# Gate and up projections of twelve feed-forward units in pairs: seven outer products over both token shares, each an inner set of seven on quarters

## The chip, the core and the metric

One core of a Trainium2 chip runs the whole decoder layer in one launch. The metric is the device time of that launch in microseconds (us), the median of several runs. TensorE (PE in the profile) multiplies matrices, VectorE (DVE) and ScalarE (ACT) work on what it leaves in PSUM, and SyncE (SP) issues nearly all DMAs from one queue in order.

## The reference

The input `x` has 2 sequences of 512 tokens of width 1024, all float32. With `ln` for a layer norm, the layer computes

```
x = ln(x + attention(x))      # 32 query heads, 8 key/value heads of 128, sliding window of 128
x = ln(x + fake_quant(x) @ fake_quant(ctx))        # "cross": ctx is 1024 x 1024 for each sequence
gate, up = (x/128) @ w_gate.T, (x/128) @ w_up.T    # 2752 hidden rows
inter = trunc(clip(silu(gate) * up * 128, -128, 127))
out = ln(x + trunc(clip((inter @ w_down.T) * 128, -128, 127)))
```

## The kernel before

**Stages.** The profile shows three. From 0 to about 790 us are the q, k and v projections and attention, for one key/value head group `g` after another (8 groups, some 98 us each). From 790 to 1170 us is the output projection (`project_out`), with the cross stage behind it. From 1170 us to the end is `feed_forward`.

**Strassen sets.** Each large projection is done by `strassen`: a 2x2 block product in seven products instead of eight. `left` holds seven weight factors (blocks and sums of blocks), `right` seven activation factors. A `product` is a chain of four matmuls (`KH` = 4 chunks of 128 of the inner dimension, 256 columns each) into one PSUM bank. The seven are made in the order 1, 5, 6, 2, 7, 4, 3 in four banks, `one` to `four`, and combined by four ACT copies and three DVE adds, of which the last, of `c12`, frees the bank `three` that the second product of the next set writes.

**Feed-forward units.** The hidden rows are cut into 21 units `m` of 128 and a rest of 64. The 1024 tokens are cut into two shares of 512 (`SHARES`: first the later tokens of both sequences, then the earlier ones). The loop takes the 22 units on share 0, then the 22 on share 1. For a unit on a share one Strassen set gives gate and up (the two block rows are the gate rows and the up rows of the unit, the two block columns are halves of the share); `activate` makes the whole-numbered activations on ACT and DVE; `split` (ACT) and `rest_of_split` (DVE) cut the down weights into two parts `hi` and `lo`, so that `down` can run in the one-pass format fp32r; and `down` adds two units (share 0) or four (share 1) to `acc` by matmuls of 512 columns and one DVE add per token tile and half. The last eight units are held and projected at the end.

**Background work in attention.** The weight factors that are sums do not depend on the tokens. A generator (`ahead`) makes them during attention and writes them to HBM: `sum_output_weights` for the output weights (32 steps) and `sum_weights` for gate and up (42 steps). A step reads 512 KB into a `room`, does four DVE operations of 256 columns, and writes 512 KB. `in_attention` is called 52 times per head group and lets one step go every third call, from the fortieth call on (`credit`).

**Background work in the feed-forward.** The cross stage of share 1 (`cross_tokens(1)`: layer norm, quantising, transposes, 16 bf16 matmuls, layer norm and transposes for each of four token tiles) lies beside the units of share 0, one step at every second `between` call. There are seven such calls per unit.

**Order.** Within the order in which the code asks for them, a list scheduler places instructions on each engine by their readiness, except where `keep_in_program_order` pins one. The engines run their queues in order.

Of the kernel before, what the change touches and what calls it, by code (L numbers as in the profile page):

```python
# [49 lines left out]
SHARES = (LATE, EARLY)  # L50

# [57 lines left out]
def strassen_left(nc, tc, pool, w, name):  # L109


    a11, a12, a21, a22 = (w[:, h, ts(k, KH)] for h in range(2) for k in range(2))
    s = pool.tile([P, 3, KH, P], F32, tag="s", name=name)
    s1, s2, s4 = (s[:, k] for k in range(3))
    tc.keep_in_program_order(nc.vector.tensor_tensor(s1, a21, a22, ALU.add))
    nc.vector.tensor_tensor(s2, s1, a11, ALU.subtract)
    nc.vector.tensor_tensor(a21, a11, a21, ALU.subtract)
    nc.vector.tensor_tensor(s4, a12, s2, ALU.subtract)
    return a11, a12, s4, a22, s1, s2, a21


def strassen(nc, psum, work, left, right, outs, name, seeded=True):
# [6 lines left out]
    def product(ps, k, start):  # L129
        for c in range(KH):  # L130
            nc.tensor.matmul(ps, left[k - 1][:, c, :], right[k - 1][:, c, :],  # L131
                             start=start and c == 0, stop=c == KH - 1, skip_group_check=True)
# [74 lines left out]
def attention(nc, tc, consts, xbuf, tpool, wpool, psum, dram, kept, complete, between):  # L207
# [3 lines left out]
    with ExitStack() as ctx:  # L211
# [9 lines left out]
        weights, lefts, right, x = {}, {}, {}, {}  # L221
# [11 lines left out]
        def load_weight(n):  # L233
            g, j = divmod(n, PAIRS)
            w = wpool.tile([P, 2, KC, P], F32, tag="w", name=f"w_{n}")
# [5 lines left out]
        def prepare(n):  # L241
            lefts[n] = strassen_left(nc, tc, wpool, weights[n], f"s_{n}")
# [12 lines left out]
        weights[0] = wpool.tile([P, 2, KC, P], F32, tag="w", name="w_0")  # L255
# [223 lines left out]
def project_out(nc, tc, xres, stream, rooms, psum, more, kept, complete, wo_d, sums):  # L479
# [9 lines left out]
    def load_left(n):  # L489
        if n < len(steps):  # L490
            k, g, bs = steps[n]
            for b in bs:
                left = lefts[n, b] = stream.tile([P, 7, P], F32, tag="left", name=f"ol_{b}_{n}", bufs=6)
# [38 lines left out]
    def held(n, t=False):  # L532
# [3 lines left out]
        if t:  # L536
            where = ("t0", n) if n < 5 else ("s", 0) if n == 5 else ("w", 0)
        tag, k = where
        if tag not in places_held:
            size = {"x0": 4 * 4 * HQ, "x1": 3 * 4 * HQ, "t0": 5 * 3 * HQ}.get(tag, 3 * HQ)  # L540
# [221 lines left out]
def load_factors(nc, pool, gate_up, m, name):  # L762

    wgu_d, rest_d, sums = gate_up
    w = pool.tile([P, 4, KH, P], F32, tag="w", name=f"wgu_{name}")
    if m == NCHUNK:
        rest = w[:, 0:2].rearrange("p a c i -> p (a c) i")
        nc.sync.dma_start(out=rest, in_=rest_d)
        return rest
    s = pool.tile([P, 3, KH, P], F32, tag="s", name=f"sgu_{name}")  # L770
# [7 lines left out]
def feed_forward(nc, tc, ident, xres, spill, x2T, xbuf, tpool, wpool, left, right, gate_up, wd_d, pools, psum, ps_p, ps_d, out, between, finish_between):  # L778

    one_pool, raw_pool, b_work = pools  # L780
    with ExitStack() as ctx:
        work = ctx.enter_context(tc.tile_pool(name="c_work", bufs=2, side="right", reuse_waits="tile"))
        inter = ctx.enter_context(tc.tile_pool(name="c_inter", bufs=3, side="right", reuse_waits="tile"))
        wdp = ctx.enter_context(tc.tile_pool(name="c_wd", bufs=3, side="right", reuse_waits="tile"))
        sums_room = tpool.tile([P, TPB, D], F32, tag="t1", name="acc")

        PER = NCHUNK + 1
        HELD = 8
        units = [(b, m) for b in range(B) for m in range(PER)]
        held_from = len(units) - HELD  # L790
        acc, raw, halves, acts = {}, {}, {}, {}

        def load_unit(u):
            if u < len(units) and u not in left:
                left[u] = load_factors(nc, wpool, gate_up, units[u][1], u)

        def load_down(u):
            if u == len(units):
                return
            m = units[u][1]  # L800
            w = raw[u] = wdp.tile([P, D], F32, tag="wd", name=f"wd_{u}", bufs=1)
# [5 lines left out]
        def split(u):  # L807


            slot = (u - PER) % 8 if u >= PER else 0  # L810
            if slot in (3, 4):

                if slot == 3:
                    room_x.append(xbuf.tile([P, 4, D], F32R, tag="x0", name=f"halves_{u}"))
                hi, lo = (room_x[-1][:, 2 * (slot - 3) + k] for k in range(2))
            else:
                places = [(wdp, "hi"), (wdp, "lo")]
                if slot == 5:
                    places = [(one_pool, "base_1"), (raw_pool, "raw")]
                elif slot > 5:  # L820
                    places = [(one_pool, f"a2_1_{2 * slot - 12 + k}") for k in range(2)]
                hi, lo = (pool.tile([P, D], F32R, tag=tag, name=f"{name}_{u}")
                          for name, (pool, tag) in zip(("hi", "lo"), places))
            first = nc.scalar.copy(hi, raw[u])
            if u >= PER:
                tc.keep_in_program_order(first)
            halves[u] = (hi, lo)

        def rest_of_split(u):
            hi, lo = halves[u]  # L830
            last = nc.vector.tensor_tensor(lo, raw[u], hi.bitcast(F32), ALU.subtract)
            if u >= PER:
                tc.keep_in_program_order(last)

        def activate(u, g, up):

            if u < PER:
                act = acts[u] = inter.tile([P, N], F32R, tag="act", name=f"act_{u}")
            else:
                place = (u - PER) % 8  # L840
                if place % 2 == 0:
                    acts["two"] = one_pool.tile([P, 2, N], F32R, tag=f"a2_0_{place // 2}", name=f"act_{u}")
                act = acts[u] = acts["two"][:, place % 2]

            a = work.tile([P, N], F32, tag="a", name=f"sg_{u}")
            nc.scalar.activation(a, g, AF.Sigmoid, scale=1.0 / 128.0)
            nc.vector.tensor_tensor(g, g, a, ALU.mult)
            nc.vector.scalar_tensor_tensor(g, g, 1.0 / 128.0, up, ALU.mult, ALU.mult)
            nc.vector.tensor_scalar(g, g, -128.0, 127.0, ALU.max, ALU.min)

            a = work.tile([P, N], F32, tag="a", name=f"mag_{u}")
            r = work.tile([P, N], F32, tag="r", name=f"rnd_{u}", bufs=1)
            nc.scalar.activation(a, g, AF.Abs)
            nc.scalar.activation(g, g, AF.Sign)
            nc.vector.tensor_scalar(r, a, RND, RND, ALU.add, ALU.subtract)
            nc.vector.tensor_tensor(a, r, a, ALU.is_gt)
            nc.vector.tensor_tensor(r, r, a, ALU.subtract)
            nc.vector.tensor_tensor(act, r, g, ALU.mult)

        def gate_up_tiles(u):  # L860
            return [work.tile([P, N], F32, tag=tag, name=f"{tag}_{u}") for tag in ("g", "u")]

        def rest_unit(u, b):

            g, up = gate_up_tiles(u)
            nc.gpsimd.memset(g[REST:], 0.0)
            nc.gpsimd.memset(up[REST:], 0.0)
            ps = ps_p.tile([P, N], F32, tag="p", name=f"rest_{u}")
            for c in range(KC):
                nc.tensor.matmul(ps, left[u][:, c], x2T[b][:, c], start=c == 0, stop=c == KC - 1)  # L870
            nc.scalar.copy(g[:REST], ps[:REST])
            nc.scalar.copy(up[:REST], ps[REST:])
            activate(u, g, up)

        def down_parts(ps, us, i, part, start, stop):
            parts = [(acts[v], half) for v in us for half in halves[v]]
            for k, (act, half) in enumerate(parts):
                nc.tensor.matmul(ps, act[:, ts(i, P)], half[:, part],  # L878
                                 start=start and k == 0, stop=stop and k == len(parts) - 1)

        def down(us, i, e):

            b, m = units[us[0]]
# [411 lines left out]
```

## Time and profile before

| | |
|---|---|
| runs | 1899.28 us median of 3 (1898.52 to 1899.99) |
| profiled execution | 1900.18 us, of which the span from first to last instruction is 1898.5 us |
| granted TensorE clock | 0.998 of full speed |
| PE, PEld, DVE, ACT busy | 1870.0, 1548.8, 1202.4, 608.6 us |
| DMA | 362.32 MB, mean 191 GB/s |

Busy time of PE counts each matmul from its start to the modelled end of its pipeline, so that neighbours overlap; the distance from one start to the next says more. PEld is the weight load ahead of a matmul. In a row of groups stand the line, the engine, the operation, output and inputs by their names in the program, the count, the busy time and the mean of one, and then the idle time of the engine ahead of it with what ended it.

### The profile page before, as it was taken

What the parts mean: (1) busy time and instruction counts of PE and PEld (TensorE: products, weight loads), DVE (VectorE), ACT (ScalarE), POOL (GpSimd) and SP (SyncE); (2) the same over time, 40 slices, a digit from 0 to 9 for tenths busy, and PEclk for the clock granted to TensorE, in tenths of its full rate; (3) what the DMA queues carried; (4) which work ended last, traced back from release to release, by engine and by line L of the source; (5) the groups of instructions that cost most, each with busy time, mean ns of one, the idle gap of its engine ahead of it and who ended that gap; (6) DMA issues with size and microseconds to landing.
All of it is one profiled execution on the core that took longest, in us unless ns stands there. A gap on an engine that the chain in (4) does not pass through costs nothing.

```text
span 1898.5 us, 24182 instructions
## 1 busy us (share of the span) xinstructions
PE 1870.0 (99%) x8678; PEld 1548.8 (82%) x8678; DVE 1202.4 (63%) x2533; ACT 608.6 (32%) x1736; POOL 13.7 (1%) x32
## 2 busy tenths in 40 slices
PE   8999999999999999999999999999999999999997
PEld 6888788888788888778888878878888878888885
DVE  3356777677775454655657776777665687544557
ACT  1334333334334343420101112334322255322334
POOL 0000000000000000000000000000000000000000
PEclk9999999999999999999999999999999999999999
DMA  5136888787974132489878663333434345543431
GB/s 187 58 119 230 299 273 301 257 299 267 310 262 162 61 142 87 160 309 318 306 262 296 216 206 131 137 125 131 144 125 169 115 164 196 189 146 128 172 131 45
DMA packets 168344, 362.32 MB, mean 191 GB/s; under 512 B 15008, under 2 KB 92064, under 8 KB 168224
## 3 DMA queue, kind: packets, MB, share of 16 engines
q1 hardware_dynamic: 165632, 356.31, 54.2%
q10 hardware_dynamic: 2592, 4.46, 0.6%
q8 instruction: 69, 1.13, 0.2%
q14 instruction: 51, 0.42, 0.1%
HBM read 264.24 MB, written 96.47 MB: 190 GB/s over the span
## 4 chain that ended last, share of the span: by engine, by line
PE 82%; DVE 10%; DMA 4%; ACT 2%; issue 1%; SPq 0%; DVEq 0%; ACTq 0%
PE prod L131 48%; PE y L603 16%; PE d L878 7%; PE ps L360 3%; PE o L419 2%; PE o L420 2%; PE pt L396 1%; DMA xT<-in_xT_dram 1%; DMA sums<-sum 1%; PE m L746 1%; DVE factors L430 1%; ACT s L384 1%; PE o L417 1%; DMA fin_x<-spill 1%; DVE ln_stats L80 1%
## 5 line engine op out<-in xcount | busy, mean ns | idle before, releaser
L603 PE MATMUL y<-or,ol 128*128 128x256 f32 x784 | 202.8, 380 | 0.0
L131 PE MATMUL prod<-xT,w 128*128 128x256 f32 x752 | 182.3, 379 | 0.0
L131 PE MATMUL prod<-t,s 128*128 128x256 f32 x752 | 178.1, 380 | 0.0
L131 PE MATMUL prod<-t,w 128*128 128x256 f32 x752 | 171.9, 379 | 0.9 <-DVE st L137 0.9
L603 PEld LDWEIGHTS y<-or,ol 128*128 128x128 f32 x784 | 148.2, 190 | 21.9 <-DVE yw L563 0.6
L131 PEld LDWEIGHTS prod<-t,w 128*128 128x128 f32 x752 | 141.6, 190 | 26.1 <-issue 7.2
L131 PE MATMUL prod<-x2T,wgu 128*128 128x256 f32 x672 | 159.5, 379 | 0.6 <-ACT g L156 0.6
L603 PE MATMUL y<-ot,ol 128*128 128x256 f32 x588 | 159.4, 379 | 0.0
L131 PEld LDWEIGHTS prod<-xT,w 128*128 128x128 f32 x752 | 138.6, 190 | 22.3 <-issue 6.5
L131 PEld LDWEIGHTS prod<-t,s 128*128 128x128 f32 x752 | 138.3, 190 | 21.8 <-issue 6.7
L131 PE MATMUL prod<-t,wgu 128*128 128x256 f32 x672 | 153.9, 379 | 0.3 <-ACT st L151 0.3
L131 PE MATMUL prod<-t,sgu 128*128 128x256 f32 x672 | 152.5, 379 | 0.4 <-ACT prod L142 0.4
L131 PEld LDWEIGHTS prod<-x2T,wgu 128*128 128x128 f32 x672 | 127.6, 190 | 19.1 <-ACT g L156 1.1
L131 PEld LDWEIGHTS prod<-t,wgu 128*128 128x128 f32 x672 | 127.3, 190 | 18.9 <-ACT st L151 0.7
L131 PEld LDWEIGHTS prod<-t,sgu 128*128 128x128 f32 x672 | 127.1, 190 | 18.8 <-ACT prod L142 0.8
L603 PEld LDWEIGHTS y<-ot,ol 128*128 128x128 f32 x588 | 111.3, 190 | 14.9
L878 PE MATMUL d<-hi,act 128*128 128x512 f32 x256 | 108.2, 423 | 0.5 <-DVE acc L889 0.4
L384 ACT ACTIVATE s<-s,top 128x128 f32<-128x128 f32 x256 | 99.5, 390 | 28.3 <-DVE top L381 27.9
L891 DVE TENSOR_TENSOR acc<-d,acc 128x512 f32<-128x512 f32 x104 | 71.6, 691 | 50.7 <-PE d L878 50.6
L878 PE MATMUL d<-lo,act 128*128 128x512 f32 x256 | 102.9, 402 | 0.0
L360 PEld LDWEIGHTS ps<-kT,qT 128*128 128x128 f32 x512 | 82.3, 190 | 17.8 <-DVE s L374 6.8
L360 PE MATMUL ps<-kT,qT 128*128 128x160 f32 (+4 forms) x512 | 92.1, 294 | 2.1 <-DVE s L374 1.7
(214 smaller groups left out, 2808.2 us busy)
## 6 DMA issues: line engine op xcount, KB each, us to landing
kept<-factors SPq DMA_DIRECT2D x112, 448.0 KB, 3.2
ol<-kept SPq DMA_DIRECT2D x112, 448.0 KB, 4.4
sgu<-sums SPq DMA_DIRECT2D x42, 768.0 KB, 6.2
room<-in_wgu_dram SPq DMA_DIRECT2D x84, 256.0 KB, 4.1
wgu<-in_wgu_dram SPq DMA_DIRECT2D x42, 512.0 KB, 3.9
wd<-in_wd_dram SPq DMA_DIRECT2D x42, 512.0 KB, 3.2
w<-in_wq_dram SPq DMA_DIRECT2D x32, 512.0 KB, 4.2
room<-in_wo_dram SPq DMA_DIRECT2D x64, 256.0 KB, 4.3
```

What stands on the lines that cost most here:

```text
L80: nc.vector.bn_stats(stats[:, h, :], x[:, ts(h, HALF)])
L131: nc.tensor.matmul(ps, left[k - 1][:, c, :], right[k - 1][:, c, :], start=start and c == 0, stop=c == KH - 1, skip_group_check=True)
L360: nc.tensor.matmul(ps[:, k, cut // BLOCK : G + 1].rearrange("p d w -> p (d w)"), qT[b, g][:, G * i + c].rearrange("p h w -> p (h w)"), kT[ ...
L384: nc.scalar.activation(s[:, h, :], s[:, h, :], AF.Exp, bias=top[:, h : h + 1], scale=QSCALE, accum_out=total[:, h : h + 1],)
L396: nc.tensor.transpose(ps[:, :, ts(c, BLOCK)], s[:, c, :], ident)
L417: nc.tensor.matmul(ps, v[b, g][:, 0, :], cur, start=True, stop=True)
L419: nc.tensor.matmul(ps, v[b, g][:, i - 1, :], both, start=True, stop=False)
L420: nc.tensor.matmul(ps, vd[b, g][:, i - 1, :], cur, start=False, stop=True)
L430: tc.keep_in_program_order(nc.vector.tensor_tensor(s1, a21, a22, ALU.add))
L603: nc.tensor.matmul(bank[:, half], left[:, SLOT[j]], mine[j], start=grow[k][0] and g == 0 and half == 0, stop=g == LAST, skip_group_check=True,
L878: nc.tensor.matmul(ps, act[:, ts(i, P)], half[:, part], start=start and k == 0, stop=stop and k == len(parts) - 1)
L891: nc.vector.tensor_tensor(acc[t][:, ts(e, HALF)], ps, acc[t][:, ts(e, HALF)], ALU.add)
```

## The change

Nine units (`SINGLE`) and the rest unit stay as they were, one share at a time: all ten on share 0 first (named a0 to a9), and the same ten on share 1 at the end (c0 to c9). Between them the other twelve units run as six pairs over both shares. The outer 2x2 product has the two units of a pair as block rows, halves of the width of 1024 as inner blocks, and the two shares as block columns. Each of its seven products (`OUTER`, in the order 1, 2, 6, 7, 4, 5, 3) is itself a Strassen set, whose products now have two matmuls of 256 columns (`KH // 2` chunks) instead of four. The results of the seven sets are combined by seven DVE adds of 1024 columns for a pair (`rest`), and sets 2, 4, 5 and 3 end in the activation of one unit on one share. Down projections of a pair are laid between the products of four of the seven sets (`queue`).

What goes with it: the right factors of both levels are made once from both shares (`joint_right`: four DVE operations of 2048 columns and 28 of 512, of which 24 lie in the first pair). The left factors of a pair, 49 blocks, are made in attention (`joint_sums`, two steps of reading per pair, with four DVE operations of 512 and four of 896 columns each) and stored with 512 bytes to a piece; `JointLeft` loads 896 KB of them for each set. `ahead` now has 50 single steps and 12 joint ones that are spread over eight calls of the generator each, of which four also do a single step, so 98 or 99 steps in all; one goes every 2.5 calls (`credit` in half units). The cross stage of share 1 takes a step at each `between` call instead of every second, since it must end before the pairs begin. Down projections of share 1 go by two units instead of four.

```diff
+SINGLE = list(range(9))
+PAIRS = [(m, m + 1) for m in range(9, NCHUNK, 2)]
+OUTER = (1, 2, 6, 7, 4, 5, 3)
+HELD = 8
...
+def weights_place(pool, name):
+
+    t = pool.tile([P, 28 * P], F32, tag="w", name=name)
+    return t[:, : 16 * P], t[:, 16 * P :].rearrange("p (k c i) -> p k c i", k=3, c=KH)
...
-        for c in range(KH):
+        chunks = left[k - 1].shape[1]
+        for c in range(chunks):
             nc.tensor.matmul(ps, left[k - 1][:, c, :], right[k - 1][:, c, :],
-                             start=start and c == 0, stop=c == KH - 1, skip_group_check=True)
+                             start=start and c == 0, stop=c == chunks - 1, skip_group_check=True)
...
+class JointLeft:
+
+
+    def __init__(self, nc, pool, joint):
+        self.nc, self.pool, self.joint = nc, pool, joint
+        self.order = [(p, o) for p in range(len(PAIRS)) for o in OUTER]
+        self.places, self.ready = None, []
+
+    def load(self):
+        n = len(self.ready)
+        if n == len(self.order):
+            return
+        p, o = self.order[n]
+        if n % 2 == 0:
+            self.places = self.pool.tile([P, 28 * P], F32, tag="w", name=f"joint_{n}")
+        place = self.places[:, ts(n % 2, 14 * P)].rearrange("p (k c i) -> p k c i", k=7, c=KH // 2)
+        self.nc.sync.dma_start(out=place, in_=self.joint[p][:, o - 1])
+        self.ready.append([place[:, k] for k in range(7)])
...
+def joint_right(nc, spill, x2T, tpool, room):
+
+
+    more = lambda out, y, z: nc.vector.tensor_tensor(out, y, z, ALU.subtract)
+    b11, b21 = (x2T[0][:, ts(k, KH)] for k in range(2))
+    b12, b22 = (x2T[1][:, ts(k, KH)] for k in range(2))
+    jt = room.tile([P, 3, KH, N], F32, tag="jt", name="jt")
+    js = room.tile([P, 13, KH // 2, NH], F32, tag="js", name="js")
+    t1, t2, t4 = (jt[:, k] for k in range(3))
+    nc.sync.dma_start(out=spill, in_=x2T[1])
+    more(t1, b12, b11)
+    yield
+    more(t2, b22, t1)
+    yield
+    more(t4, b21, t2)
+    yield
+    more(b12, b22, b12)
+    yield
+    jr = tpool.tile([P, 8, KH // 2, NH], F32, tag="t0", name="jr")
+    places = [jr[:, k] for k in range(8)] + [js[:, k] for k in range(13)]
+    outer = {1: b11, 2: b21, 3: b22, 4: t4, 5: t1, 6: t2, 7: b12}
+    factors = {}
+    q = KH // 2
+
+    def inner(o):
+        f = outer[o]
+        c11, c12, c21, c22 = (f[:, ts(k, q), ts(n, NH)] for k in range(2) for n in range(2))
+        s1, s2, s4 = (places[3 * OUTER.index(o) + k] for k in range(3))
+        factors[o] = c11, c21, c22, s4, s1, s2, c12
+        return (s1, c12, c11), (s2, c22, s1), (s4, c21, s2), (c12, c22, c12)
+
+    yield factors, {o: [lambda a=a: more(*a) for a in inner(o)] for o in OUTER}
...
+        queue = {1: todo[:4], 2: todo[4:]}
+        doing = []
+
+        def proceed():
+            while doing:
+                try:
+                    return next(doing[0])
+                except StopIteration:
+                    doing.pop(0)
+
+        add = lambda out, y, z: nc.vector.tensor_tensor(out, y, z, ALU.add)
+        mine = {}
+        for p, (m, m2) in enumerate(PAIRS):
+            final = p == len(PAIRS) - 1
+            for slot, o in enumerate(OUTER, 1):
+                n = 7 * p + slot - 1
+                name = f"j{p}_{o}"
+                tag, bufs = {1: ("w1", 1), 6: ("w2", 1)}.get(o, ("gu", 3))
+                x, outs = gate_up_tile(name, tag, bufs)
+                mine[o] = x
+                to_do = queue.pop(slot, [])
+                following = sums[OUTER[slot]] if p == 0 and slot < 7 else []
+                for k, _ in enumerate(strassen(nc, psum, work, stream.ready[n], factors[o], outs, name)):
+                    if k in (0, 1, 2, 4, 5):
+                        proceed()
+                    if k in (1, 2, 4, 5) and to_do:
+                        down(*to_do.pop(0))
+                    if k in (1, 2, 3, 4) and following:
+                        following.pop(0)()
+                    if k == 3:
+                        stream.load()
...
+                    if slot == 3 and k == 0:
+                        load_down(f"m{m}", m)
+                    elif slot == 4 and k == 3:
+                        split(f"m{m}")
+                    elif slot == 4 and k == 4:
+                        rest_of_split(f"m{m}")
+                    elif slot == 4 and k == 5:
+                        load_down(f"m{m2}", m2)
+                    elif slot == 5 and k == 3:
+                        split(f"m{m2}")
+                    elif slot == 5 and k == 4:
+                        rest_of_split(f"m{m2}")
...
+                def rest(o, name, mine=dict(mine)):
+                    x = mine[o]
+                    if o in (6, 7, 4, 3):
+                        add(x, x, mine[{6: 1, 7: 6, 4: 7, 3: 6}[o]])
+                    elif o == 2:
+                        add(x, x, mine[1])
+                    elif o == 5:
+                        add(mine[6], mine[6], x)
+                        add(x, x, mine[7])
+                    yield
+                    if o in (2, 4, 5, 3):
+                        act = acts[name] = inter.tile([P, N], F32R, tag="act", name=f"act_{name}")
+                        yield from activation(name, x[:, 0], x[:, 1], act)
+
+                doing.append(rest(o, name))
+                if slot == 6:
+                    first = downs([(f"j{p}_2", f"m{m}"), (f"j{p}_4", f"m{m2}")], 0)
+                    second = downs([(f"j{p}_3", f"m{m}"), (f"j{p}_5", f"m{m2}")], 1)
+                    queue = {7: first[:4], 1: first[4:], 2: second[:4], 3: second[4:]}
...
+    def joint_sums(p, k):
+
+        f = sums_pool.tile([P, 7, 2, 2, P], F32, tag="f", name=f"joint_f_{p}_{k}")
+        for u, m in enumerate(PAIRS[p]):
+            for j in range(2):
+                for h in range(2):
+                    src = wgu[m, :, h].rearrange("p (j q k) i -> p j k q i", j=2, q=2)
+                    nc.sync.dma_start(out=f[:, (0, 1, 6, 3)[2 * u + j], h], in_=src[:, j, k])
+        for _ in range(4):
+            yield False
+        b = sums_pool.tile([P, 3, 7, P], F32, tag="b", name=f"joint_b_{p}_{k}")
+        pin = lambda out, y, z, op: tc.keep_in_program_order(nc.vector.tensor_tensor(out, y, z, op))
+        a11, a12, s4, a22, s1, s2, a21 = (f[:, o].rearrange("p h q i -> p (h q i)") for o in range(7))
+        pin(s1, a21, a22, ALU.add)
+        nc.vector.tensor_tensor(s2, s1, a11, ALU.subtract)
+        yield True
+        pin(a21, a11, a21, ALU.subtract)
+        nc.vector.tensor_tensor(s4, a12, s2, ALU.subtract)
+        yield True
+        a11, a12, a21, a22 = (f[:, :, h, q] for h in range(2) for q in range(2))
+        s4, s1, s2 = (b[:, n] for n in range(3))
+        pin(s1, a21, a22, ALU.add)
+        nc.vector.tensor_tensor(s2, s1, a11, ALU.subtract)
+        yield True
+        pin(a21, a11, a21, ALU.subtract)
+        nc.vector.tensor_tensor(s4, a12, s2, ALU.subtract)
+        to = joint[p]
+        for n, src in enumerate((a11, a12, s4, a22, s1, s2, a21)):
+            nc.sync.dma_start(out=to[:, :, n, k], in_=src)
+        yield True
+
+    def all_sums():
+
+        rest = single_sums()
+        for p in range(len(PAIRS)):
+            for k in range(2):
+                for joint_step in joint_sums(p, k):
+                    if not joint_step:
+                        next(rest, None)
+                    yield
+        yield from rest
...
+    credit = [-80]
 
     def in_attention(b, g, i, lump, keeping):
         last = b and g == NKV - 1
-        if last and ahead.queue:
+        if g == NKV - 1 and ahead.queue:
             ahead.drain()
-        if last and credit[0] % 2 == 0 or (b, g) == (0, NKV - 1) and len(begun) < i - 1:
+        if last and credit[0] % 4 == 0 or (b, g) == (0, NKV - 1) and len(begun) < i - 1:
             begun.append(next(output))
-        credit[0] += 1
+        credit[0] += 2
         if lump:
             pass
         elif keeping.queue:
             keeping.step()
-        elif credit[0] >= 3 and ahead.queue:
-            credit[0] -= 3
+        elif credit[0] >= 5 and ahead.queue:
+            credit[0] -= 5
...
-    aside.add(cross_tokens(1), 2)
...
+    def joint_steps():
+        cross_stack.close()
+        joint_rooms.append(joint_stack.enter_context(tc.tile_pool(name="joint", bufs=1, reuse_waits="tile")))
+        making.append(joint_right(nc, x2T_spill, x2T, tpool, joint_rooms[0]))
+        for _ in range(4):
+            next(making[0])
+            yield
+
+    aside.add(cross_tokens(1))
+    aside.add(joint_steps())
```

## Prediction

> **What bounds the kernel now.** I read first the page, then the groups, the chain of waits, the windows, PE's own waits and the order of events around one down projection.
>
> ```profile
> PE 1870.0 (99%) x8678; PEld 1548.8 (82%) x8678; DVE 1202.4 (63%) x2533; ACT 608.6 (32%) x1736; POOL 13.7 (1%) x32
> ...
> L131 PE MATMUL prod<-x2T,wgu 128*128 128x256 f32 x672 | 159.5, 379 | 0.6 <-ACT g L156 0.6
> ...
> L891 DVE TENSOR_TENSOR acc<-d,acc 128x512 f32<-128x512 f32 x104 | 71.6, 691 | 50.7 <-PE d L878 50.6
> ```
>
> PE waits for almost nothing, but 379 ns for a matmul is not its price. The chain shows steps, by stages:
>
> ```profile
> 414.89 10.36 PE prod L131 x48
> 514.30 10.36 PE prod L131 x48
> 614.22 10.36 PE prod L131 x48
> 712.40 10.36 PE prod L131 x48
> 1347.11 7.77 PE d L878 x32
> 1788.46 12.09 PE prod L131 x56
> ```
>
> A whole set of a unit on a share is 56 instructions in 12.09 us, 0.216 us each; a product of four matmuls is eight of them, 1.73 us. A down matmul costs 0.243 us (7.77 / 32). A head group of attention lasts 99.4 to 99.9 us with background work and 98.2 without. Nothing but PE's own work fills these stretches: a matmul less is time less, as long as what the other engines owe PE comes in time.
>
> ```profile
> 150.00:600.00 450.00, 443.92 (x2115) 365.43 (x2114) 321.36 (x792) 175.01 (x705) 4.73 (x9) 1.00 0.82 275
> 600.00:790.00 190.00, 189.42 (x901) 156.96 (x900) 96.61 (x213) 72.64 (x295) 2.10 (x4) 1.00 0.28 106
> 1170.00:1520.00 350.00, 349.28 (x1614) 287.81 (x1613) 234.38 (x413) 117.37 (x205) 1.93 (x3) 1.00 0.39 135
> 1520.00:1600.00 80.00, 78.02 (x335) 62.47 (x334) 64.42 (x116) 45.84 (x70) 0.00 (x0) 1.00 0.55 194
> ```
>
> Columns are PE, PEld, DVE, ACT, POOL busy, clock, DMA share, GB/s. The clock is full. While sums are made (150 to 600) DMA is at 0.82 and DVE at 71%; afterwards DMA falls to 0.28. In the feed-forward DVE is at 67%, at the change of shares at 80%.
>
> ```profile
> DVE sum L1144 <- DMA sums<-sum: 7.1, 5, 2.3
> PEld d L878 <- DVE acc L891: 13.1, 55, 0.3
> ```
>
> These two waits, of the whole run and of 1170 to 1850, are what there is of the kind that the change adds.
>
> **Matmuls (gain).** Twelve units on two shares are 24 sets of 56: 290.2 us. The six pairs are 42 sets of 28: 42 x 28 x 0.216 = 254.0. So 336 instructions go, **-36.3 us**. All else is what is paid for it.
>
> **Waits in the pairs.** A product now lasts 0.86 us, not 1.73, and the answers keep their length.
>
> ```profile
> 1317.63 0.39 PE L878 MATMUL d<-lo,act 128*128 128x512 f32 x1
> 1317.88 0.19 PEld L878 LDWEIGHTS d<-hi,act 128*128 128x128 f32 x1 [0.29 <-DVE acc L891]
> 1318.05 0.69 DVE L891 TENSOR_TENSOR acc<-d,acc 128x512 f32<-128x512 f32 x1 [0.23 <-PE d L878]
> ```
>
> DVE starts 0.03 us after the modelled end of a matmul (0.19 after PE's step), and PE 0.06 after DVE. For the last add of a set (`c12`, 0.42 us in L137) that is 0.19 + 0.42 + 0.06, and some 0.1 to restart: 0.78 us until the next set's second product may write its bank. In the built program's order the next set's first product (0.86) covers that where down projections lie between. In the three sets without them one has nothing between and two have half a product (0.43): 0.78 + 0.35 + 0.35, and 0.7 for adds that stand behind an activation's operation in DVE's queue: 2.2 us per pair. DVE's work per pair is 21 adds x 0.42, 7 x 1.22 (as L831), 4 activations x 4.30 (seven operations of 0.43 and 0.69), 16 x 0.69 and 2 x 1.22: 48.1 us, beside 42.3 + 64 x 0.243 = 57.9 us of PE. Set by set it exceeds PE in sets 6 and 7 of a pair, by 0.75 and 0.83 us, if each operation takes its whole duration; independent operations follow each other 0.09 us sooner (L664, L858, L665 at 1313.04, 1313.64, 1314.24), and then nothing is exceeded. Bounds 0 and 3.8 (both) per pair; I take 2.2, the counted waits: **+13**.
>
> The Trainium skill ("Trainium Kernel Development and Optimization", Best Practices) speaks against the change: packing more into TensorE does not speed up emptying PSUM. Sets go from 24 to 42, each with three adds of 0.42 and four ACT copies of 0.37, so 49 us more of emptying; were none of that hidden, the sum would end at a loss of 13 us before other terms. In the rows PE's wait for such a copy or add is 0.3 to 1.0 us in the whole stage, so I go by the counted waits.
>
> **First pair.** 24 operations of 512 columns more, 14 us of DVE, in sets of which four have no down projections (6.05 us of PE): DVE needs 8.5, 5.7, 5.7, 8.5 there. **+5**; between 0 and 9 (all at full durations).
>
> **Down projections.** Before, groups of eight stood in a row and waited for `acc` (the 13.1 us above); against 0.216 a step they lose 0.86 us in share 0 and some 0.57 in share 1 (61 in 14.26 us in the chain), 8.6 for the twelve units. Now they lie between products. **-5**, between 0 and -8.6. The 24 adds more (16.6 us of DVE) are in the sum per pair.
>
> **Units a0 to a5.** The cross steps come at double pace. A token tile costs DVE 11.8 us in ten steps, so 8.3 per unit; with the unit's own 9.6, 17.9 us against PE's 12.1 + 3.9 + 3.5 = 19.5. Before it was 13.7. **+3** for what collides, 0 to 10. The four operations of 2048 columns (2.3 us each, by the slope of L137, L891 and L831) fall into units a6 to a8 where the cross steps are over.
>
> **Change of shares.** The dip at 1520 goes, two smaller changes come (28 operations are spread): **0**, -6 to +6. The set loads, 896 KB each 6 to 10 us, are about 110 GB/s where 135 to 152 ran; they are asked for two sets ahead, and 768 KB took 6.2 us to land.
>
> **Attention.** Joint sums are 12 x (4 x 0.69 + 4 x 1.09) = 85 us of DVE instead of 40: 71% becomes about 79%. DMA matters more. The packet records of the trace have 1024-byte packets at 51 ns (76,544, mean) and 512-byte ones at 29 (256). Before: 74 steps of 1024 packets = 241 us on 16 engines, in 74 x 3 calls x 1.9 us = 422 us; 0.57 + 0.28 = 0.85, as the window has it. After: 50 x 1024 packets (163 us) and 12 x 8320 of 512 bytes (182 us), 345 us in 99 x 2.5 x 1.9 = 470 us: 0.73 + 0.28 = **1.01**. By the medians (46 and 27 ns) it is 0.94. DMA will be full, and behind a late DMA stand SP's stores of `kept`, its weight loads, and DVE's pinned sums. At 0.82 DVE waited 10 us for it, and the background cost 1.2 us per head group. I take twice these 5 us and 3 for DVE: **+8** net of what is paid now. Below: 0, as rooms are four deep. Above: at 0.92 of the engines the 477 us of DMA take 518, +45.
>
> The skill's "DMA: Bandwidth & Descriptors", Specifications, lets pieces from 512 bytes on run at line rate. Then the joint part would cost 51.1 MB at the rate of 1024-byte packets, 159 us, and the share be 0.96. The row (17.6 against 20.1 bytes per ns) is worse, and I use it.
>
> **Sum.** -36.3 + 13 + 5 - 5 + 3 + 0 + 8 = -12. From the profiled 1900.2 us (span 1898.5 and 1.7 around it) to 1888; the median of the runs is 0.9 below the profile: **1887 us**.
>
> **Rivals.** *DMA full in attention.* Sums arrive late, DVE's queue stops at them, PE follows. At 0.95 the 477 us become 502, +32 instead of +8: **1911**. It decides from a stretch of some 20 us on. For: 1.01, and one buffer for `joint_f`, whose loads wait for its stores in SP's queue. Against: stretches of the trace with DMA at 0.97 for 20 us without a halt of PE. *DVE bounds the pairs:* full durations, 3.8 per pair and 9 in the first, no gain in the down projections: +10 + 4 + 5, **1906**. For: four sets in seven have an activation beside the down adds. Against: 83% at most on the whole. *Nearly all waits hidden:* pairs +4, first +2, units +1, attention +3, down -7: **1866**. For: the scheduler puts half of the next set's products ahead. That the matmuls do not go is excluded by the built program, which has 336 fewer.
>
> **How the numbers follow.** Forecast 0.43, own range 1878 to 1898; DMA 0.25; DVE 0.18; hidden 0.14. A measurement here tells 0.2% (3.8 us) from no change. Faster: 0.37 of the forecast and the 0.14. Same: 0.04 of the forecast, 0.02 of each slow rival. Slower: 0.02, 0.23, 0.16. The range 1868 to 1918 leaves out half of the hidden case and the upper ends of the slow ones.
>
> **What would show it.** Head groups near 101 us until about 640 us and DMA at 0.95 or more: right; 104 or more, with DVE waiting on `joint_f` or sums: the first rival. Pairs of about 60 us and 64 for the first: right; 63 and more with PE waiting on L147 of DVE: the second. I am wrong in kind if the singles lose over 10 us or PE waits for `joint` loads.

## The result, and the profile after

The changed kernel took 1904.3 us (median of 20 runs, 1898.5 to 1909.6) where the kernel before took 1899.6 in the same rounds: a ratio of 1.0026 (95% interval 1.0018 to 1.0035), 4.7 us slower. The forecast was 1887. Its profiled execution is the longest of the 20 (1909.6 us, span 1907.9), so stages are told from that span, and sizes are taken from the medians of the experiments.

The first `y` matmul and the first product of the feed-forward divide the span into the three stages. PE in the order of time, of the kernel after:

```profile
806.54 0.60 PE L615 MATMUL y<-held_x,ol 128*128 128x256 f32 x2
...
1213.98 1.89 PE L141 MATMUL prod_a<-x2T,wgu 128*128 128x256 f32 x8
```

Before, the same two began at 785.97 and 1169.69.

| stage | before | after | difference | forecast |
|---|---|---|---|---|
| up to the first `y` | 786.0 | 806.5 | +20.6 | +8 |
| to the first feed-forward product | 383.7 | 407.4 | +23.7 | 0 |
| to the end | 728.8 | 693.9 | -34.9 | -20.3 |

The gain in the feed-forward is larger than forecast, attention lost more, and a stage to which the sum gave no loss lost as much as attention. Windows of the kernel after show each (columns: window and its length; then the busy time of PE, PEld, DVE, ACT and POOL; clock, DMA share, GB/s). An engine "stands" where it is idle:

```profile
150.00:650.00 500.00, 481.44 (x2277) 393.37 (x2276) 378.67 (x829) 187.37 (x754) 5.25 (x10) 1.00 0.94 300
820.00:870.00 50.00, 33.75 (x109) 21.74 (x108) 28.27 (x67) 10.77 (x46) 0.00 (x0) 0.73 0.55 205
1214.00:1907.90 693.90, 678.30 (x3071) 562.08 (x3073) 544.97 (x974) 272.18 (x506) 3.87 (x6) 1.00 0.40 144
```

The same windows of the kernel before:

```profile
150.00:650.00 500.00, 493.87 (x2350) 407.35 (x2349) 345.77 (x844) 193.13 (x776) 5.25 (x10) 1.00 0.76 256
800.00:850.00 50.00, 48.80 (x222) 39.19 (x222) 28.88 (x66) 11.64 (x50) 0.00 (x0) 1.00 0.83 308
1169.70:1898.50 728.80, 715.18 (x3243) 593.06 (x3241) 470.50 (x834) 261.96 (x448) 3.81 (x6) 1.00 0.40 141
```

In the first row PE stands 18.6 us; before, in the same 500 us, 6.1. In the last, PE's busy time is 36.9 us less than the 715.2 before, which is the matmuls that went: 168 of them (PE's weight loads in the whole trace, one for each, are 8510 after and 8678 before). The middle row is the surprise: at the end of attention PE stands 16 of 50 us and its clock averages 0.73 (before: 48.8 us busy, clock 1.00). What PE waited for there (us in total, times, longest), after:

```profile
PE y L615 <- DVE held_t L535: 7.8, 2, 7.3
PE o L431 <- ACT both L415: 4.4, 2, 2.9
PE pt L408 <- DVE s L386: 2.2, 1, 2.2
```

These are the waits of the last head group's own chain of scores, softmax and weighing; the longest, 7.3 us, is for a sum of output weights (`held_t`), which DVE makes only when it is through with that chain. Before, PE filled them with `y` matmuls: 106 instructions of them stand ahead of the last `o` in the trace before, 40 in the trace after.

### The profile page after: what moved, and what is told of

Read it like the earlier page. It is cut to its first block, busy times and chain, and to the rows that moved or that the text cites. A ratio compares the mean times of both kernels' runs of the same rounds, so it can differ in the third digit from the quotient of the medians.

```text
span 1907.9 us, 23992 instructions
## 1 busy us (share of the span) xinstructions
PE 1847.3 (97%) x8500; PEld 1523.0 (80%) x8510; DVE 1317.4 (69%) x2673; ACT 617.9 (32%) x1794; POOL 13.7 (1%) x32
## 4 chain that ended last, share of the span: by engine, by line
PE 72%; DVE 14%; DMA 7%; SPq 3%; ACT 2%; issue 2%; DVEq 0%; ACTq 0%
PE prod L141 17%; PE y L615 16%; PE prod_j L141 13%; PE prod_c L141 5%; PE d_j L924 5%; PE prod_a L141 3%; PE ps L372 2%; PE d_a L924 2%; PE o L431 2%; DMA joint<-joint_f 1%; PE o L432 1%; SPq L1355 1%; PE pt L408 1%; PE m L758 1%; ACT s L396 1%
## 5 line engine op out<-in xcount | busy, mean ns | idle before, releaser
L141 PE MATMUL prod<-t,w 128*128 128x256 f32 x1504 | 352.9, 381 | 2.5 <-DVE st L147 2.5
L141 PEld LDWEIGHTS prod<-t,w 128*128 128x128 f32 x1504 | 280.9, 191 | 50.9 <-issue 14.4
L141 PE MATMUL prod<-xT,w 128*128 128x256 f32 x1128 | 270.2, 382 | 8.7 <-DVE qT L147 5.7
L141 PEld LDWEIGHTS prod<-xT,w 128*128 128x128 f32 x1128 | 210.0, 191 | 46.7 <-issue 8.3
L141 PE MATMUL prod_j<-x2T,joint 128*128 128x256 f32 x384 | 94.7, 379 | 0.0
L924 PE MATMUL d_j<-hi_m,act_j 128*128 128x512 f32 x192 | 92.4, 481 | 0.0
L141 PEld LDWEIGHTS prod_j<-x2T,joint 128*128 128x128 f32 x384 | 72.6, 190 | 12.3 <-DVE w_j L147 0.3
L924 PE MATMUL d_j<-lo_m,act_j 128*128 128x512 f32 x192 | 78.7, 410 | 0.0
L141 PE MATMUL prod_j<-js,joint 128*128 128x256 f32 x312 | 78.3, 380 | 0.0
L141 PE MATMUL prod_j<-jt,joint 128*128 128x256 f32 x288 | 71.8, 380 | 0.1
L936 DVE TENSOR_TENSOR acc<-d_j,acc 128x512 f32<-128x512 f32 x88 | 59.6, 683 | 10.7 <-PE d_j L924 10.0
```

What stands on the lines that cost most here:

```text
L924: nc.tensor.matmul(ps, act[:, ts(i, P)], half[:, cols], start=start and k == 0, stop=stop and k == len(terms) - 1)
L936: nc.vector.tensor_tensor(acc[t][:, ts(e, HALF)], ps, acc[t][:, ts(e, HALF)], ALU.add)
```

## Experiments

Eleven kernels ran, in three sets, each five rounds against the kernel before.

| run | us | ratio to before (95%) |
|---|---|---|
| e1_steps | 1881.5 | 0.9903 (0.9890 to 0.9917) |
| e2_before_no_steps | 1922.4 | 1.0121 (1.0105 to 1.0137) |
| e3_no_stores | 1870.3 | 0.9846 (0.9832 to 0.9859) |
| e4_half_sums | 1880.1 | 0.9904 (0.9888 to 0.9921) |
| e5_pace | 1874.9 | 0.9869 (0.9853 to 0.9884) |
| e6_pieces | 1873.1 | 0.9858 (0.9842 to 0.9874) |
| e7_extra_sums | 1893.4 | 0.9965 (0.9952 to 0.9977) |
| e8_pace_pieces | 1867.7 | 0.9831 (0.9815 to 0.9846) |
| e9_four_deep | 1873.8 | 0.9863 (0.9848 to 0.9877) |
| e10_all | 1866.6 | 0.9828 (0.9814 to 0.9841) |
| e11_extra_five | 1884.4 | 0.9920 (0.9907 to 0.9933) |

### The steps that were lost

`in_attention` steps the output projection in the last head group whenever `credit[0] % 4 == 0`, and adds 2 to the credit at every call. The background takes 5 at a time. It is asked 99 times: 12 joint parts of eight steps, the two single steps left over, and the call that finds the list at its end. So -80 + 2n - 495 is odd, and the condition can never hold. Before, the credit went up by 1 and every second call was a step.

**e1_steps**

```diff
-        if last and credit[0] % 4 == 0 or ...
+        if last and credit[0] % 4 < 2 or ...
```

> The changed kernel with one comparison altered: in the last head group the output projection is stepped where the credit modulo 4 is 0 or 1, not 0 alone. Theory 'lost steps': the pace takes 5 from the credit 99 times (98 steps and the one that finds the list at its end), so the credit is odd in the last head group, goes up by 2, and is never a multiple of 4; the projection gets no step there, PE has no y matmuls beside the last scores. In the profile of the changed kernel PE stood 16.7 us in 800 to 870 (before, in 770 to 850, 1.7) and its clock was at 0.5 for 24 us. With the steps back both go: 1904 becomes 1880 to 1884, and PE's idle time in that place is under 3 us. Rival 'SP queue': the loads of the left factors (ol) stand in SP's queue behind the stores of kept and two residual loads that took 9.5 us to issue; the comparison doesn't move them past these, so the time stays within 4 us of 1904.

1881.5: the 22.8 us are back, all of the second stage's loss (the first `y` at 802.27, the first product at 1185.84: 383.6 us, before 383.7). The same window in its profile:

```profile
820.00:870.00 50.00, 48.82 (x223) 39.52 (x222) 28.25 (x72) 11.59 (x47) 0.00 (x0) 1.00 0.86 315
```

PE is busy for 48.8 us as before, at the full clock.

**e2_before_no_steps**, the same loss put into the kernel before:

```diff
-        if last and credit[0] % 2 == 0 or (b, g) == (0, NKV - 1) and len(begun) < i - 1:
+        if (b, g) == (0, NKV - 1) and len(begun) < i - 1:
```

> The kernel before, with the condition for steps of the output projection in the last head group taken out (the steps in the first share of it stay). Theory 'lost steps': the loss is this alone and needs nothing else of the change: 1899.5 becomes 1917 to 1924, with PE idle for some 15 us around 800 to 835 and the clock at half in the same place. Rival 'SP queue' (the loss comes of the joint sums' leftovers and the new room for the left factors): within 4 us of 1899.5.

1922.4, 23 us more. PE's waits in 790 to 875 of its profile have the signature of the changed kernel, to the tenth for all but the first:

```profile
PE y L603 <- DVE held_t L523: 7.3, 1, 7.3
PE o L419 <- ACT both L403: 4.4, 2, 2.9
PE pt L396 <- DVE s L374: 2.2, 1, 2.2
```

So nothing else of the change is needed for this loss, and the queue of SP (its residual loads and stores of `kept`) does not make it: the order of the `ol` loads there, late in the changed kernel (813.69, then 863.82), goes with the missing steps (e1_steps issues them at 809.42, 823.07, 830.54 and on). Some 15 us are PE's idle time. The rest goes with the clock, which the record of the trace has at one half for 27.3 us there in the kernel after (3.41 and 23.89) and for 30.7 in e2_before_no_steps (6.83 and 23.89); PE worked in about 17 of the 27.3, so some 8 us is an estimate of what that cost.

### What attention lost: DMA or DVE

**e3_no_stores** and **e4_half_sums** take from e1_steps the one and the other. (The first also lets the loads of all six pairs read the sums of pair 0.)

```diff
-            nc.sync.dma_start(out=to[:, :, n, k], in_=src)
+            if p == 0:
+                nc.sync.dma_start(out=to[:, :, n, k], in_=src)
```

> As e1_steps, but the joint sums of pairs 1 to 5 are not written to DRAM (70 of 84 stores left out; their loads read pair 0's, so the output is another). DVE's work is the same. That takes 10 x 6272 packets of 512 bytes, at 29 ns on 16 engines 114 us of DMA time, out of 150 to 650, where the share was 0.96: it becomes about 0.74. Theory 'DMA full in attention': of the 20.5 us that attention lost in the profile 10 to 16 come back, 1882 becomes 1866 to 1872. Rival 'DVE's queue' (85 us of joint sums, in operations of up to 1.1 us that stand ahead of the scores' and products' operations): within 4 us of e1_steps.

```diff
-        s4, s1, s2 = (b[:, n] for n in range(3))
-        pin(s1, a21, a22, ALU.add)
-        nc.vector.tensor_tensor(s2, s1, a11, ALU.subtract)
+        s4, s1, s2 = a12, a21, a22
         yield True
-        pin(a21, a11, a21, ALU.subtract)
-        nc.vector.tensor_tensor(s4, a12, s2, ALU.subtract)
```

> As e1_steps, but without the inner four of the eight joint operations of each step (12 x 4 x 1.09 = 52 us of DVE's 85; raw slices are stored in their place, so the output is another). The DMA is the same, byte for byte. DVE is then at about 67 to 70% in 150 to 650, as before the change. Theory 'DMA full in attention': within 4 us of e1_steps, with the DMA share still 0.95 or more. Rival 'DVE's queue': 10 to 16 us less than e1_steps, 1866 to 1872. If both this and e3_no_stores gain about half of that, it is the two together.

Without the stores 11.2 us came back, with DVE's work as it was; without 52 us of DVE's work 1.3, which is no difference here. The same window of e1_steps, of e3_no_stores, and then of e4_half_sums:

```profile
150.00:650.00 500.00, 483.96 (x2281) 394.84 (x2280) 380.21 (x834) 189.13 (x760) 4.72 (x9) 1.00 0.95 303
```

```profile
150.00:650.00 500.00, 493.01 (x2336) 405.13 (x2335) 385.70 (x842) 191.12 (x769) 5.24 (x10) 1.00 0.73 243
```

```profile
150.00:650.00 500.00, 484.90 (x2291) 398.03 (x2290) 336.81 (x786) 188.30 (x759) 4.73 (x9) 0.99 0.96 306
```

With DMA at 0.73 PE stands 7.0 us though DVE is at 77%; with DMA at 0.96 it stands 15.1 though DVE is at 67% (e1_steps: 16.0, with 0.95 and 76%). In this window it is the DMA. The whole of attention does not come back with the stores: the first `y` of e3_no_stores is at 792.16, 6 us later than before the change, and what keeps these 6 us was not taken apart.

The longest case in the trace of the kernel after shows how it gets to PE, first on DVE and then on PE:

```profile
203.29 0.68 DVE L392 TENSOR_REDUCE top<-s 128x4 f32<-128x512 f32 x1
206.92 0.42 DVE L1309 TENSOR_TENSOR wo_sum<-room 128x256 f32<-128x256 f32 x1 [2.96 <-DMA wo_sums<-wo_sum]
...
212.55 0.42 DVE L147 TENSOR_TENSOR vT<-prod,st 128x256 f32<-128x256 f32 x1
```

```profile
206.71 3.62 PE L141 MATMUL prod<-t,w 128*128 128x256 f32 x16
213.02 3.35 PE L141 MATMUL prod<-xT,w 128*128 128x256 f32 x7 [2.69 <-DVE vT L147]
```

A pinned sum waits 2.96 us for a store, because its result goes into one of two buffers (`sums`, two deep) whose store is late; the attention's own work queues behind it, the add of `vT` comes late, and PE stands 2.69 us for the bank. (The seven instructions after it take 3.35 us, not 1.51: half the clock.)

### Three ways out, and the sum of them

**e5_pace**: one step per 6 of credit.

```diff
-        elif credit[0] >= 5 and ahead.queue:
-            credit[0] -= 5
+        elif credit[0] >= 6 and ahead.queue:
+            credit[0] -= 6
```

> As e1_steps, but a background step is taken for every 6 of credit, not 5: every third call, not every 2.5 calls. The same 333 us of DMA time of the sums (0.96 less 0.28 of 490 us) are spread over 99 x 3 x 1.9 = 564 us: a share of 0.28 + 0.59 = 0.87. DMA theory: e3_no_stores, at 0.70 to 0.77, gained 11 us; this one gains 6 to 9, to 1873 to 1876, and the background ends near 725 us in place of 645. Rival 'bursts': the calls that go to the stores of kept leave their credit standing, and the sums that follow come three in a row (DVE at 195.0, 197.1 and 206.9 us, the third 3 us late behind the second's store); a slower pace leaves these bursts as they are, and the time stays within 3 us of e1_steps.

**e6_pieces**: the order of the joint sums in HBM and of their tile.

```diff
-    joint = [scratch.tile([P, 7, 7, 2, P], ...
+    joint = [scratch.tile([P, 2, 7, 7, P], ...
-        f = sums_pool.tile([P, 7, 2, 2, P], ...
+        f = sums_pool.tile([P, 2, 2, 7, P], ...
-            nc.sync.dma_start(out=to[:, :, n, k], in_=src)
+            nc.sync.dma_start(out=to[:, k, n], in_=src)
...
-        self.nc.sync.dma_start(out=place, in_=self.joint[p][:, o - 1])
+        self.nc.sync.dma_start(out=place, in_=self.joint[p][:, :, :, o - 1])
```

> As e1_steps, but the joint sums lie in DRAM so that each of the 84 stores writes 3584 bytes in a piece where it wrote seven of 512; in return each of the 42 loads of a joint set reads 512 bytes at a time, not 7168. In the packet records 512 bytes took 29 ns (17.6 bytes per ns) and 3584 took 155 ns (23). The stores cost 12 x 896 x 155 / 16 = 104 us, not 137: of 333 us of the sums' DMA 33 go and the share is 0.89. DMA theory, by packets: 3 to 6 us gained, 1876 to 1879; the feed-forward, at 0.35, doesn't feel its smaller pieces. Rival, by bytes alone (the queue is full of bytes, not of packets): no gain, within 2 us of e1_steps, and the share stays at 0.95.

**e9_four_deep**: nothing less for DMA or DVE to do, only more buffers.

```diff
+    def sums_tile(shape, name):
+        turn = next(turns) % 4
+        return (stream if turn % 2 else sums_pool).tile(shape, F32, tag="sums", name=name, bufs=2)
...
-        t = stream.tile([P, 3, Q4], F32, tag="sums", name=f"wo_sum_{g}_{j}_{q}", bufs=2)
+        t = sums_tile([P, 3, Q4], f"wo_sum_{g}_{j}_{q}")
```

> As e1_steps, but the results of the output and single gate and up sums lie in four buffers by turns, not two; DMA and DVE do the same work at the same pace. In e1_steps (150 to 740) DVE waited 25.2 us for DMA: 11.5 for a buffer whose store was not through (sums<-sum 5.9, wo_sums<-wo_sum 4.7 and 0.9), 12.7 for loads of room, 1.0 for a weight. Theory 'short buffers' (a full DMA reaches PE by way of the two buffers): the 11.5 go, and of attention's loss 4 to 6 us: 1876 to 1878. Rival 'DMA itself': the engines are full all the same, the wait goes over to the loads and to joint_f, and the time is within 2 us of e1_steps.

From the 1881.5 of e1_steps the pace gained 6.5 us (1874.9, as expected), the pieces 8.4 (1873.1; more than the 3 to 6 expected), the buffers 7.6 (1873.8; more than the 4 to 6). Bursts and bytes alone are out as causes: the pace did change it, and the same bytes in larger packets cost less. Rows of 400 to 640 us of e1_steps, e5_pace, e6_pieces and e9_four_deep, in this order:

```profile
400.00:640.00 240.00, 232.18 (x1093) 188.25 (x1092) 185.73 (x407) 89.80 (x361) 2.14 (x5) 1.00 0.96 306
```

```profile
400.00:640.00 240.00, 235.19 (x1109) 192.09 (x1108) 177.03 (x385) 90.69 (x364) 2.10 (x4) 0.99 0.86 275
```

```profile
400.00:640.00 240.00, 236.14 (x1121) 193.72 (x1120) 184.78 (x404) 93.19 (x375) 2.10 (x4) 1.00 0.92 318
```

```profile
400.00:640.00 240.00, 233.67 (x1097) 190.23 (x1096) 180.68 (x392) 90.42 (x362) 2.10 (x4) 0.99 0.98 313
```

The pace lowers the DMA share to what was worked out for it (0.87). The pieces lower it while more bytes pass per second. The last row is the instructive one: DMA is fuller than in e1_steps, and yet PE stands 10.3 us in 150 to 640, not 16.0. DVE's waits for a store of results (11.5 us in e1_steps, in 150 to 740) are gone; those for loads of `room` remain, 14.8 us, and are a likely source of the rest of the loss.

Not every such wait of DVE reaches PE. In e5_pace DVE waits 15.7 us for stores of results in 150 to 740, more than in e1_steps, and not at all for `room`, and PE stands 9.9 us in 150 to 640. So the two buffers are one way from a full DMA to PE, and e9_four_deep sizes it; the sum of DVE's waits does not.

The pieces also cost something. In return for the larger stores the loads of a joint set read 512 bytes at a time, and the left factors lie in another order in their tile. With the pieces the feed-forward lasts 697.2 to 697.7 us (the profiles of e6_pieces, e8_pace_pieces and e10_all); in the kernel after and the five others that add nothing to the pairs it lasts 693.7 to 694.6. So it does feel them, by some 3 us, against what was expected; the 8.4 us are what is left after that. Which of the two makes it was not tried.

**e8_pace_pieces** has the pace and the pieces, **e10_all** the buffers too.

> e5_pace and e6_pieces together. DMA theory: 300 us of the sums over 564 us, a share of 0.28 + 0.53 = 0.81, what the kernel before had (0.82): nearly all of what e3_no_stores gained, 11 to 13 us, 1868 to 1871. Rival 'bursts': no more than 4 us, 1877 or above.

> e8_pace_pieces with the four buffers of e9_four_deep. In e8_pace_pieces DVE waited 8.7 us for such stores and PE stood no longer in 150 to 640 than before the change (5.0 us against 6.1). Theory 'nothing is left there': within 2 us of e8_pace_pieces, 1866 to 1869. Theory 'short buffers': 2 to 4 us less, 1864 to 1866.

1867.7 and 1866.6: as expected, and no difference between the two that these runs can tell. e10_all is 1.72% faster than the kernel before (1.59 to 1.86), the best version found. Its row:

```profile
400.00:640.00 240.00, 239.03 (x1135) 197.29 (x1135) 182.44 (x392) 91.57 (x366) 2.10 (x4) 1.00 0.81 285
```

PE stands 1.0 us of 240 (the kernel before: 2.4), and the first `y` comes at 782.96, 3 us sooner than before the change (half of that may be spread: in e2_before_no_steps, whose attention is the old one up to there, it came at 784.61).

### How far DVE was from setting the pace of the pairs

**e7_extra_sums** and **e11_extra_five** (the latter with the number of extra additions 0 in the last pair):

```diff
+                    for _ in range(2):
+                        add(spare, x[:, 0], x[:, 1])
                     if o in (2, 4, 5, 3):
```

> As e1_steps, with two more additions of 512 columns (0.69 us each, into a spare tile that nobody reads) behind each of the 42 sets of the pairs: 9.7 us more of DVE per pair, 44.0 of 57.3 us busy becomes about 53. It asks how far DVE was from setting the pace of the pairs, where the prediction counted 2.2 us of waits per pair and the trace has none. Theory 'room': the order has half of the next set's products ahead, so DVE may be late by a product or two; up to 53 of 57.3 it costs at most 0.7 us per pair, 4 in all: 1881 to 1886. Rival 'just covered': an answer that comes 1.4 us later is 1.4 us more for the set that has no down projection behind it, some 3 x 1.4 + 2.2 per pair: 1905 or more.

> As e7_extra_sums, but the additions behind the sets of the first five pairs only, 70 of 84. In e7_extra_sums the pairs took as long as in e1_steps (activation to activation 284.5 us against 284.2 for five), and 10.7 us were lost behind the last pair, where DVE was at 58.5 of 60 us busy (54.9 in e1_steps) and the residual's loads, sums and stores follow one another in one buffer. Theory 'the last pair': DVE has room in five pairs and none in the sixth, which also makes the second share's sums; the loss goes, 1881 to 1885. Rival 'order': more DVE work anywhere changes the order behind the pairs or leaves DVE behind there, and 1890 or more stays.

e7_extra_sums took 1893.4, 12 more, between what the two theories allowed. A window within the pairs, and the stretch behind them, of e1_steps and then of e7_extra_sums:

```profile
1490.00:1550.00 60.00, 60.00 (x273) 51.06 (x272) 46.07 (x78) 20.48 (x45) 0.00 (x0) 1.00 0.37 139
...
1718.00:1840.00 122.00, 120.63 (x534) 100.33 (x533) 82.52 (x154) 59.49 (x96) 1.93 (x3) 1.00 0.56 194
```

```profile
1490.00:1550.00 60.00, 59.88 (x273) 51.09 (x272) 54.97 (x92) 20.38 (x44) 0.00 (x0) 1.00 0.39 141
...
1718.00:1840.00 122.00, 115.59 (x514) 97.31 (x513) 81.64 (x153) 57.81 (x92) 0.99 (x2) 0.99 0.56 192
```

With DVE busy for 55 of 60 us PE lost 0.1: in the steady pairs there is room for nearly all of 9 us more. Not for quite all: from the first activation of the pairs to the first one of the last pair it is 284.6 us, in e1_steps 282.7 (not the 284.2 that the expectation of e11_extra_five names), so each pair is some 0.4 us longer. Behind them PE stands 6.4 of 122 us where it stood 1.4 in e1_steps. Without the additions of the last pair the time was 1884.4 and that stretch was as in e1_steps:

```profile
1718.00:1840.00 122.00, 120.64 (x537) 100.65 (x536) 83.26 (x156) 58.92 (x96) 1.93 (x3) 1.00 0.56 194
```

So 9 of the 12 us belong to 14 additions in the last pair, where DVE was at 92% already (1660 to 1720 of e1_steps) and where, in the chain of e7_extra_sums, the loads, sums and stores of the residual follow one another through one buffer, `x_end`; that this buffer is the reason was not tried. The 3.0 us that the other 70 cost are within the range expected for "room".

## Why the prediction was wrong

The forecast was 12 us faster; the kernel is 4.7 us slower.

**The step that failed is one that the sum did not have.** The output projection's stage was taken as unchanged, and it lost 23.7 us (22.8 by e1_steps, 23 by e2_before_no_steps). The prediction costed what the change adds and moves, but did not follow the arithmetic of the credit through the one other line that reads it. It needed no chip to see: the pace of 5 and the test for a multiple of 4 stand in one function of the diff. None of the rivals has this mechanism; the second one's 1906 (DVE bounds the pairs) lies nearest the result, and what it names did not happen.

**Attention, +8: mis-sized, 15 to 21.** It is 20.6 in the span after and 16.3 in that of e1_steps, which has the same code up to there; e7_extra_sums and e11_extra_five, again the same, have 15.4 and 18.0. DMA did become full (0.94 to 0.96; forecast 1.01, 0.94 by the medians; the working gave 0.85 for the kernel before, where its row has 0.82), which was the first rival's mechanism; e3_no_stores and e4_half_sums show it against DVE. Five head groups in a row took 102.7 us each (first transpose of `vT` to the next group's, 113.79 to 627.46; before 99.8), between the 101 of the forecast and the 104 of the rival, whose +32 was too much. The bound "0, as rooms are four deep" looked at the wrong buffer: the rooms hold what is loaded, and the longest halt was at the two buffers of results. (Waits of DVE for `joint_f`, which the rival names first, are not in the trace after.) e9_four_deep shows 7.6 us of the loss to be that. At the start 2.3 us went: a set began at 31.72, before at 29.41. SP issues eight loads of `joint_f` just ahead of that (from 10.44 on), where it issued `room` before; that these are the reason was not tried.

**Matmuls, -36.3:** right (PE busy 36.9 us less). The count beside it is not: 24 sets of 56 less 42 of 28 are 168 matmuls, which at 0.216 us are the 36.3, and not 336.

**Waits in the pairs, +13, and the first pair, +5: nothing.** PE's waits of 1433 to 1715 in the trace after are none, and the pairs lasted 57.2 to 57.5 us in e1_steps against 57.9 of counted matmuls. The count assumed one or two products between an answer and the bank that needs it; with answers later by up to 1.4 us (two additions) in every set a pair was only some 0.4 us longer (e7_extra_sums), so there was more cover than that. The third rival named it ("the scheduler puts half of the next set's products ahead"); that this is the reason was not tried apart. The skill ("Trainium Kernel Development and Optimization", Best Practices) warns that tiling TensorE speeds up its work but not the emptying of PSUM. No such limit shows here: of an estimated 49 us more of copies and adds, PE waited 0.5 us for one in the pairs of e1_steps.

**Down projections -5, units a0 to a5 +3, change of shares 0:** about right as far as they can be told apart. In e1_steps PEld's waits of `d` for `acc` (L936, before L891) are 4.6 us, before 13.1, and PE's idle time in the first nine units of share 0 is 2.8, before 0.7; the change of shares was not measured by itself. In the whole feed-forward PE stands 15.6 us in the trace after, before 13.6: +2 where these terms and the waits had +16.

**The DMA price per packet held.** 29.2 ns for 512 bytes in the trace after, and e6_pieces shows that the rate is what counts: 3584 bytes took 153 ns, 23.4 bytes per ns against 17.5. The skill's "DMA: Bandwidth & Descriptors", Specifications, has pieces from 512 bytes on at line rate; the runs differ, since storing the same bytes in larger pieces gave 8.4 us.

So forecast and result agree in no stage. With the lost steps given back the kernel takes 1881.5, and the forecast of 1887 would have been near by luck, with two errors against each other: attention 7 to 13 us too low, the feed-forward 15 too high.

## What to carry to other kernels

When a pace or a counter changes, look for every other place that reads it, and count the filler work in the built order ahead of the stage's end; work that is merely not interleaved is not in any sum of added and removed operations. When background transfers fill the DMA engines, the price appears where an in-order engine waits for a buffer, so look first at the shallowest buffer on the way out, then at the size of the pieces, then at the pace. Larger pieces on one side of a transfer can mean smaller ones on the other, so time both sides. An engine's average says little about the place where it decides: with DVE at 92% a steady pair lost some 0.4 us of 57, and as many additions in the last pair cost 9.

## What the hardware showed that was not expected

The record of the granted clock has its half-speed stretches during the work in lengths of 3.41 us and multiples (6.83, 23.89). They came behind idle times of PE as short as 1.86 us (e9_four_deep, ended at 425.2), 1.90 (e7_extra_sums, 1763.5), 2.07 (e1_steps, 210.8) and 2.69 (the kernel after, 213.0), while 2.38 us that ended at 24.6 of e1_steps and 2.94 at 242.7 of e6_pieces had none behind them. In the stretch with the lost steps one lasted 23.89 us, in which PE stood for several waits of 0.7 to 7.3 us. The skill's "TensorE: Matmul & The Clock Gate", Part 1, gives free-running windows of 3.4 us and half the clock after an idle window; the lengths agree, but here a gap of little more than half a window was enough.
